# First-layer norms on ScalarE as scale and shift, and the additive part's first weights prepared beside the first chosen heads

## The chip, the cores and the metric

The kernel runs on one core of one Trainium2 chip. The metric is device time of the whole kernel in microseconds (us), the median of several runs. A core has five engines that each work through their own queue in order: TensorE (PE in the profile, with PEld for its weight loads), VectorE (DVE), ScalarE (ACT), GpSimd (POOL) and SyncE (SP, which issues DMAs here).

## The reference, cut to what matters

Input `x` is 4 x 512 x 128 in float32 (B = 4 batches, 512 tokens, width 128). Six residual blocks follow each other:

```python
x = x + 0.5 * _L0_ffn_ref(_layernorm(x), ...)   # "latent": RMS norm, 16-head causal attention, then 8 experts, top 2
x = x + _L0_attn_ref(_layernorm(x), ...)        # "full": 16-head attention without a mask
x = x + 0.5 * _L0_ffn_ref(_layernorm(x), ...)   # "latent" again
x = x + 0.5 * _L1_ffn_ref(_layernorm(x), ...)   # "chosen": per head the 64 tokens it picks
x = x + _L1_attn_ref(_layernorm(x), ...)        # "additive": 4 layers of additive attention with an MLP
x = x + 0.5 * _L1_ffn_ref(_layernorm(x), ...)   # "chosen" again
```

What the change touches are norms. A latent block takes `y = layernorm(x)` and then `h = y * rsqrt(mean(y*y) + 1e-6) * g1`; a full block takes `layernorm(x)` alone; and within a latent block, before its experts, there is a second RMS norm `y * rsqrt(mean(y*y) + 1e-6) * g2`. The additive block's weights are folded before use: products such as `Wp @ Wf`, `Wq @ Wq.T` with the norm's gain and bias worked in.

## The kernel before, in words

All of `X` (and a second copy `Y`) stays in SBUF, as 128 partitions x 4 batches x 4 chunks x 128. The function `tile_macaron` calls three parts in turn: `first_layer` (the first three blocks, interleaved), `chosen_attention`, `additive_attention`, and `chosen_attention` once more.

**First layer.** There are 12 tasks: latent, full, latent, each for four batches. `attention()` walks over all their units; a unit is four groups of heads for one chunk of queries. Each unit has two halves. In a half it issues two score matmuls for the row maxima (`maxima`, L527), two in transposed form with the maximum already subtracted (`shifted`, L562), the maxima's reduction on VectorE (`reduce_max`, L543 with a mask or L547), two exponentials on ScalarE (`exponent`, L574), the causal mask on GpSimd (`mask`, L580), the products with the values two units later (`products`, L605), and one step each of an expert's first and second product (`one_hidden`, `one_combined`, L267 with ScalarE L467, VectorE L472 and GpSimd L473). Then `step_background` runs one step of whatever generator waits: the `yield`s in the code are the ends of such steps.

Two of these generators are what the change touches. `Task.prepare` (L301 to L352) makes a task's normed input: moments on VectorE (L167, L171), variance plus epsilon (L312, L316) and the power -0.5 on GpSimd (`rsqrt`, L154), a step later the norm itself, `h`, four instructions of 128 x 128, one for each chunk (L323; on VectorE for the first task, on GpSimd for all others), a step later the transposes (L193) and their copy `hT` on ScalarE (L339 or L331). A latent task also writes the plain layernorm to `Y` in four more GpSimd instructions (L336). `gates` (L673 on) is the second RMS norm of a latent task, which GpSimd applies in four instructions (L686), followed by the top-2 choice among the experts (L703 to L737, with two GpSimd steps, L712 and L718).

PSUM has eight banks of 128 x 512; `bank()` deals them out by a written-down estimate of when each will be free. The build then orders each engine's instructions itself: an instruction written later can be put ahead of an earlier one where the build's own estimate sees that engine idle and the inputs there. On the chip each queue then runs strictly in that order.

**Chosen attention** (L858 on) picks tokens with an 8-at-a-time maximum on VectorE (L836, L838), gathers them by matmuls (L880), projects (L903), attends and adds back (L983, L992). `in_turn` runs its generators round robin: the four batches' streams, and the choice for batches 2 and 3.

**Additive attention** (L1009 on) first prepares the folded weights of layer 0 to the end (`weights(0)`: six DMAs L1035 to L1045, VectorE L1049 to L1106, TensorE L1058, L1074, L1080, L1095, L1097, L1104, ScalarE L1065 and L1084), then starts four streams five turns apart; the weights of layers 1 to 3 are prepared beside the streams. Its tiles lie in pools that open after those of the chosen attention have closed.

Of the kernel before, what the change touches and what calls it, by code (L numbers as in the profile page):

```python
# [15 lines left out]
B = 4  # L16
# [24 lines left out]
def tile_macaron(ctx: ExitStack, tc: tile.TileContext, a: dict, out: bass.AP):  # L41
# [97 lines left out]
    def in_turn(runs):  # L139

        t = 0
        while runs:
            for start, run in list(runs):
                if start <= t and next(run, 0) == 0:
                    runs.remove((start, run))
            t += 1
# [85 lines left out]
    def first_layer(opened, picked):  # L232
        with (
# [42 lines left out]
            class Task:  # L276
# [24 lines left out]
                def prepare(self):  # L301
# [15 lines left out]
                    n = 2 * NC if self.causal else NC  # L317
                    r = rsqrt(v[:, 0:n], n)
                    yield
                    eng = nc.gpsimd if self.k else nc.vector  # L320
                    for c in range(NC):
                        at = n - NC + c
                        eng.tensor_scalar(  # L323
                            h[:, c, :], X[:, b, c, :], mv[:, c, 0:1], r[:, at : at + 1], ALU.subtract, ALU.mult
                        )
                    yield
                    if self.part == "full":
                        nc.gpsimd.tensor_tensor(
                            X[:, b], X[:, b], late["a_bo"].unsqueeze(1).to_broadcast([P, NC, P]), op=ALU.add
                        )  # L330
                        nc.scalar.copy(hT, transposed(h))  # L331
                        yield
                        wq, wk, self.wv, src = late["a_wq"], late["a_wk"], late["a_wv"], hT
                    else:
                        for c in range(NC):
                            nc.gpsimd.tensor_scalar(  # L336
                                Y[:, b, c, :], X[:, b, c, :], mv[:, c, 0:1], r[:, c : c + 1], ALU.subtract, ALU.mult
                            )
                        nc.scalar.activation(hT, transposed(h), AF.Copy, scale=f_cols[:, 0:1])  # L339
                        yield  # L340
                        wq, wk, self.wv, src = f_wq, f_wkv[:, 0:P], f_wkv[:, P : 2 * P], hT
                    self.src = src
                    ps = bank()
# [329 lines left out]
            def gates(task):  # L673
# [9 lines left out]
                yield  # L683
                h = wp.tile([P, NC, P], F32, name="h")
                for c in range(NC):
                    nc.gpsimd.tensor_scalar(h[:, c, :], Y[:, b, c, :], r[:, c : c + 1], None, ALU.mult)  # L686
                yield
                nc.vector.scalar_tensor_tensor(X[:, b], Y[:, b], 0.5, X[:, b], ALU.mult, ALU.add)
                yield
# [165 lines left out]
        for i, b in enumerate(batches):  # L855
            picked[b] = ygs[i], byt[:, :, i * NE : (i + 1) * NE]

    def chosen_attention(top, picked, choosing):  # L858

        with tc.tile_pool(name="moa", bufs=2) as wp:  # L860

# [135 lines left out]
            def behind(b):  # L997

                while b not in picked or (b > 0 and steps[b - 1] < 5):
                    yield  # L1000
                for _ in stream(b):
                    steps[b] += 1
                    yield
                steps[b] += 5

            in_turn([(0, choosing)] + [(0, behind(b)) for b in range(B)] + [(0, others)])


    def additive_attention(opened, picked):  # L1009

        A = 2 * P
        with tc.tile_pool(name="add", bufs=2) as wp, tc.tile_pool(name="one", bufs=1) as hp:

            fold = hp.tile([P, P], F32, name="fold")
            nc.gpsimd.affine_select(
                out=fold,
                in_=ident,
                pattern=[[0, P]],  # L1020
                compare_op=ALU.is_ge,
                fill=-1.0,
                base=P - 2,
                channel_multiplier=-1,
            )
            hs = [hp.tile([P, NC, P], F32, name=f"hs{b}") for b in range(B)]
            for b in range(B):
                nc.gpsimd.memset(hs[b][:, :, P - 1 : P], 1.0)
            ready, finished = {}, set()

            def weights(i):

                cols = late["l_cols"][:, i, :]
                wqk = wp.tile([P, 2 * A], F32, name="wqk")
                nc.sync.dma_start(wqk, a["l_wqk"][i])  # L1035
                bqk = wp.tile([P, A], F32, name="bqk")
                nc.sync.dma_start(bqk, a["l_bqk"][i, :, 0:A])
                wpT = wp.tile([P, 2, A], F32, name="wpT")
                nc.sync.dma_start(wpT, a["l_wpT"][i].rearrange("(h p) n -> p h n", p=P))
                wfg = wp.tile([P, 2, P + 1], F32, name="wfg")  # L1040
                nc.sync.dma_start(wfg, a["l_wfg"][i].rearrange("(h p) n -> p h n", p=P))
                w1 = wp.tile([P, 4 * P], F32, name="w1")
                nc.sync.dma_start(w1, a["l_w1"][i])
                w2 = wp.tile([P, 4, P], F32, name="w2")
                nc.sync.dma_start(w2, a["l_w2"][i].rearrange("(h p) n -> p h n", p=P))  # L1045
                for _ in range(3):
                    yield
                L = wp.tile([P, P], F32, name="L")
                nc.vector.tensor_scalar(  # L1049
                    L[:, 0 : P - 1], fold[:, 0 : P - 1], cols[:, COL_G1 : COL_G1 + 1], None, ALU.mult  # L1050
                )
                nc.vector.tensor_copy(L[:, P - 1 : P], cols[:, COL_B1 : COL_B1 + 1])

                wpf = wp.tile([P, 2, P], F32, name="wpf")
                ps = bank()
                for f in range(2):
                    for k in range(2):
                        nc.tensor.matmul(  # L1058
                            ps[:, f * P : (f + 1) * P],
                            lhsT=wpT[:, k, f * P : (f + 1) * P],  # L1060
                            rhs=wfg[:, k, 0:P],
                            start=(k == 0),
                            stop=(k == 1),
                        )
                nc.scalar.copy(wpf, ps[:, 0:A].rearrange("p (f n) -> p f n", f=2))  # L1065
                yield
                bpw = wp.tile([P, 2, P], F32, name="bpw")
                for f in range(2):
                    nc.vector.tensor_scalar(
                        bpw[:, f, :], wfg[:, f, 0:P], cols[:, COL_BP + f : COL_BP + f + 1], None, ALU.mult  # L1070
                    )

                ps = bank()
                nc.tensor.matmul(ps[:, 0:A], lhsT=L, rhs=wqk[:, 0:A], start=True, stop=True)  # L1074
                wq = wp.tile([P, A], F32, name="wq")
                nc.vector.tensor_tensor(wq, ps[:, 0:A], bqk, ALU.add)
                yield
                ps = bank()
                for f in range(4):
                    nc.tensor.matmul(  # L1080
                        ps[:, f * P : (f + 1) * P], lhsT=wqk[:, f * P : (f + 1) * P], rhs=L, start=True, stop=True
                    )
                wT = wp.tile([P, 4, P], F32, name="wT")
                nc.scalar.copy(wT, by_chunk(ps))  # L1084
                nc.vector.tensor_tensor(
                    wT[:, :, P - 1], wT[:, :, P - 1], cols[:, COL_BQK : COL_BQK + 4], ALU.add
                )
                yield

                wa = wp.tile([P, A + P + 1], F32, name="wa")  # L1090
                ps = bank()
                for k in range(2):
                    for f in range(2):
                        of = wT[:, 2 * k + f, :]
                        nc.tensor.matmul(ps[:, k * P : (k + 1) * P], lhsT=of, rhs=of, start=(f == 0), stop=(f == 1))  # L1095
                for f in range(2):
                    nc.tensor.matmul(  # L1097
                        ps[:, A : A + P + 1], lhsT=wT[:, f, :], rhs=wfg[:, f, :], start=(f == 0), stop=(f == 1)
                    )
                nc.vector.tensor_copy(wa, ps[:, 0 : A + P + 1])  # L1100
                yield
                ps = bank()
                for f in range(2):
                    nc.tensor.matmul(ps[:, 0:P], lhsT=ones[:, 0:P], rhs=bpw[:, f, :], start=(f == 0), stop=(f == 1))  # L1104
                crow = wp.tile([P, P], F32, name="crow")
                nc.vector.tensor_tensor(crow, ps[:, 0:P], late["l_rows"][:, i, ROW_BF : ROW_BF + P], ALU.add)  # L1106
                ready[i] = wa, wq, wT, wpf, crow, w1, w2

            def stream(b):

# [150 lines left out]
                finished.add(b)  # L1261


            for _ in weights(0):
                pass
            STEPS = 23
            runs = [(STEPS // B * b, stream(b)) for b in range(B)]
            runs += [(STEPS * (i - 1) + 15, weights(i)) for i in range(1, DEPTH)]
# [16 lines left out]
            in_turn(runs + [(STEPS * DEPTH, chosen_beside())])  # L1285
        return top, picked, choosing

    for half in (first_layer, additive_attention):
        with ExitStack() as until_chosen:

            def opened():
                return until_chosen.enter_context(tc.tile_pool(name="top", bufs=1, side="right"))

            chosen_attention(*half(opened, {}))
    for b in range(B):
        nc.sync.dma_start(out[b].rearrange("(c p) d -> p c d", p=P), X[:, b])

# [66 lines left out]
```

## Time and profile before

| | |
|---|---|
| Median of 3 runs | 1376.09 us (1375.94 to 1377.14) |
| The profiled execution's own time | 1375.36 us |
| Span of that execution, first to last instruction | 1373.6 us |
| PE busy | 1288.2 us (94%) |
| DVE busy | 953.5 us (69%) |
| ACT busy | 587.1 us (43%) |
| POOL busy | 563.3 us (41%) |
| First layer, its units | about 17 to 815 us, the last experts until about 885 us |
| First chosen attention | about 885 to 978 us |
| Additive attention | about 978 to 1250 us |
| Second chosen attention | about 1250 to 1374 us |

Times in a trace are counted from the first instruction. A row of the timeline reads: start, length, engine, line, operation, what it writes and what it reads, shapes, how many in a row, and in brackets how long the engine had been idle before and what ended that. A row of the waits reads: who waited for whom, us in total, how often, the longest. In the table of stages, PEclk is the share of its full clock that TensorE was granted.

### The profile page before, as it was taken

The page shows a single profiled execution, that of the slowest core. Times are in us where ns is not written, and L with a number is a line of the kernel's source. Part 1 is how long each engine was busy: PE and PEld are TensorE (multiplying, and loading weights), DVE is VectorE, ACT ScalarE, POOL GpSimd, SP SyncE. Part 2 cuts the span into 40 slices and gives each one's busy share as a digit, 9 for nine tenths or more (in the row PEclk, how much of TensorE's full clock was granted, in tenths as well). Part 3 has the DMA queues.
Part 4 walks back from the last instruction along what each step waited for, and adds up shares of the span by engine and source line. Part 5 has one row for each costly group of instructions (what it writes and reads, how often), then busy time and mean ns, then how long its engine had stood idle before and what let it go on. Part 6 is the DMA issues. An engine that isn't in the chain of part 4 may idle for free.

```text
span 1373.6 us, 29346 instructions
## 1 busy us (share of the span) xinstructions
PE 1288.2 (94%) x11050; PEld 699.2 (51%) x11050; DVE 953.5 (69%) x3293; ACT 587.1 (43%) x1180; POOL 563.3 (41%) x823
## 2 busy tenths in 40 slices
PE   5998999999999999999999999989799999997897
PEld 2554444333333333465444443466667767665675
DVE  6886676666657777878767548687466776667773
ACT  1555454454546666655545443222123332323122
POOL 8345655544424202025564655622144443543100
PEclk8999999999999999999999999999969999999799
DMA  3001111020111100000101021000300000000000
GB/s 115 21 24 43 40 33 49 2 80 1 64 44 32 38 2 18 18 3 19 60 22 46 20 71 40 32 0 17 100 20 5 16 1 16 1 1 1 1 9 23
DMA packets 37172, 39.52 MB, mean 29 GB/s; under 512 B 11080, under 2 KB 23880, under 8 KB 37032
## 3 DMA queue, kind: packets, MB, share of 16 engines
q1 hardware_dynamic: 34536, 35.06, 8.1%
q10 hardware_dynamic: 2496, 2.59, 0.6%
q8 instruction: 87, 1.43, 0.4%
q14 instruction: 53, 0.43, 0.1%
HBM read 29.45 MB, written 1.18 MB: 22 GB/s over the span
## 4 chain that ended last, share of the span: by engine, by line
PE 71%; DVE 17%; POOL 9%; issue 2%; ACT 1%; DMA 0%; SPq 0%; DVEq 0%; POOLq 0%; ACTq 0%
PE bank L562 17%; PE sum L605 10%; PE bank L267 10%; PE sum L267 7%; PE bank L527 6%; POOL r L154 4%; PE bank L193 4%; PE bank L880 2%; PE bank L983 2%; DVE st L167 2%; PE bank L1250 2%; PE bank L903 1%; PE bank L1142 1%; PE bank L1244 1%; DVE junk L543 1%
## 5 line engine op out<-in xcount | busy, mean ns | idle before, releaser
L574 ACT ACTIVATE e<-bank 128x512 f32<-128x512 f32 x576 | 313.9, 595 | 276.5 <-PE bank L527 238.0
L527 PE MATMUL bank<-kA,qA 32*128 32x512 f32 (+3 forms) x1536 | 345.6, 524 | 3.8 <-DVE nm L543 1.8
L562 PE MATMUL bank<-qA,kA 32*128 32x512 f32 (+3 forms) x1536 | 331.9, 521 | 0.3 <-DVE nm L543 0.3
L543 DVE CUSTOM_DVE_ANT_0 junk<-bank,causal 128x384 f32<-128x384 f32 (+3 forms) x512 | 251.0, 490 | 88.4 <-PE bank L527 50.2
L547 DVE TENSOR_REDUCE nm<-bank 128x1 f32<-128x512 f32 x256 | 164.9, 686 | 77.4 <-PE bank L527 77.0
L473 POOL TENSOR_TENSOR hid<-v,spread 128x512 f32<-128x512 f32 x128 | 164.1, 1288 | 126.0 <-DVE v L472 101.5
L562 PEld LDWEIGHTS bank<-qA,kA 32*128 32x128 f32 x1536 | 128.5, 184 | 136.6 <-issue 54.8
L605 PE MATMUL sum<-e,vA 128*32 128x256 f32 (+1 forms) x2560 | 183.1, 367 | 7.5 <-POOL e L580 7.5
L580 POOL TENSOR_SCALAR_AFFINE_SELECT e<-e 128x256 f32<-128x256 f32 x256 | 99.7, 409 | 191.3 <-ACT e L574 190.3
L527 PEld LDWEIGHTS bank<-kA,qA 32*128 32x128 f32 x1536 | 146.0, 185 | 23.8 <-DVE nm L543 5.8
L605 PEld LDWEIGHTS sum<-e,vA 128*32 128x32 f32 x2560 | 62.7, 109 | 166.5 <-issue 133.6
L267 PE MATMUL sum<-hid,sb_f_w 128*32 128x512 f32 x1024 | 135.6, 597 | 2.8 <-POOL hid L473 2.7
L267 PE MATMUL bank<-tT,sb_f_w 128*32 128x512 f32 x1024 | 137.1, 602 | 0.0
L472 DVE SCALAR_TENSOR_TENSOR v<-th,bank 128x512 f32<-128x512 f32 x128 | 87.1, 681 | 43.3 <-ACT th L467 28.4
L467 ACT ACTIVATE th<-bank 128x512 f32<-128x512 f32 x128 | 76.4, 598 | 48.5 <-PE bank L267 39.0
L154 POOL TENSOR_TENSOR r<-v,mhalf 128x4 f32<-128x4 f32 (+1 forms) x64 | 71.9, 1125 | 5.1
L1244 PE MATMUL bank<-h2T,w 128*128 128x512 f32 x128 | 69.0, 632 | 0.2 <-ACT h2T L1233 0.2
L1250 PE MATMUL bank<-w,hid 128*128 128x128 f32 x512 | 65.6, 277 | 0.1
L1250 PEld LDWEIGHTS bank<-w,hid 128*128 128x128 f32 x512 | 62.9, 194 | 4.8 <-issue 1.5
L1245 ACT ACTIVATE hid<-bank,sb_l_cols 128x512 f32<-128x512 f32 x64 | 44.0, 689 | 40.1 <-PE bank L1244 39.8
L1142 PE MATMUL bank<-wa,hT 128*128 128x385 f32 x128 | 57.6, 547 | 2.5 <-ACT hT L1135 2.5
L312 POOL TENSOR_SCALAR v<-mv 128x4 f32<-128x4 f32 x12 | 2.8, 231 | 130.8 <-DVE mv L171 130.5
(279 smaller groups left out, 1807.9 us busy)
## 6 DMA issues: line engine op xcount, KB each, us to landing
spread<-away SPq DMA_DIRECT2D x64, 256.0 KB
qA<-mT SPq DMA_DIRECT2D x192, 2.0 KB
qA<-qC SPq DMA_DIRECT2D x11, 256.0 KB
kA<-kC SPq DMA_DIRECT2D x11, 256.0 KB
w<-in_l_w_dram SPq DMA_DIRECT2D x8, 256.0 KB
sb_m_wqkv<-in_m_wqkv_dram SPq DMA_DIRECT2D x4, 384.0 KB
m_yg<-in_m_trig_dram SPq DMA_DIRECT2D x8, 130.0 KB
X<-in_x_dram SPq DMA_DIRECT2D x4, 256.0 KB
```

The source lines that it names most:

```text
L154: last_root[0] = nc.gpsimd.tensor_tensor(r[:, 0:n], src, mhalf[:, 0:n], op=ALU.pow).ins
L267: nc.tensor.matmul(ps[32 * j : 32 * j + 32, :], lhsT=w[:, 32 * j : 32 * j + 32], rhs=rhs, start=start, stop=stop, skip_group_check=True,)
L472: nc.vector.scalar_tensor_tensor(v, th, 1.0, ph, ALU.add, ALU.mult)
L473: nc.gpsimd.tensor_tensor(hid, v, self.spread[e], op=ALU.mult)
L527: nc.tensor.matmul(ps[:, at : at + w], lhsT=t.qA[r0 : r0 + 32, g, c * P : (c + 1) * P], rhs=t.kA[r0 : r0 + 32, g, 0:w], start=True, stop=True,
L543: nc.vector.tensor_tensor_reduce(junk[:, 0:w], src, causal[:, T - w : T], 1.0, NEG, ALU.add, ALU.max, dst)
L547: nc.vector.tensor_reduce(dst, src, axis=AX.X, op=ALU.max)
L562: nc.tensor.matmul(ps[:, at : at + w], lhsT=t.kA[r0 : r0 + 32, g, kc * P : (kc + 1) * P], rhs=t.qA[r0 : r0 + 32, g, q0:T], start=True, sto ...
L574: nc.scalar.activation(es[n][:, j, :], ps, AF.Exp)
L580: nc.gpsimd.affine_select(out=e, in_=e, pattern=[[0, 2], [1, P]], compare_op=ALU.is_ge, fill=0.0, base=0, channel_multiplier=-1,)
L605: nc.tensor.matmul(to[32 * j : 32 * j + 32, q0 + lo - at : q0 + hi - at], lhsT=t.vA[:, kc, 4 * j + g, :], rhs=es[n][:, j, lo:hi], start=fresh,
L1250: nc.tensor.matmul(pm[:, c * P : (c + 1) * P], lhsT=hid[:, f, c * P : (c + 1) * P], rhs=w2[:, f, :], start=(f == 0), stop=(f == 3),)
```

## The change

It does four things.

1. In `Task.prepare`, VectorE computes `nb = -mean * r` (one instruction for a full task, two for a latent one, each 128 x 4). For every task but the first, `h` is written one step later, and by ScalarE: an activation Identity with `r` as scale and `nb` as bias.
2. For latent tasks but the first, `Y` is written by ScalarE in the same way, after the step that issues `hT`.
3. In `gates`, `h = Y * r` is written by ScalarE instead of GpSimd.
4. `weights` moves out of `additive_attention` into a function of its own, `additive_weights`, with its own pool (`made`) that opens ahead of the first chosen attention; `weights(0)` runs there from turn 8, six turns between its DMAs and its first use. The tiles `wqk`, `bqk`, `wpT`, `wfg`, `L` and `bpw` have one buffer instead of two.

```diff
-                    eng = nc.gpsimd if self.k else nc.vector
+                    nb = small.tile([P, 2, NC], F32, name="nb")
+                    for i in range(n // NC):
+                        nc.vector.scalar_tensor_tensor(
+                            nb[:, i, :], mv[:, :, 0], -1.0, r[:, i * NC : (i + 1) * NC], ALU.mult, ALU.mult
+                        )
+                    def applied(dst, i, c):
+                        at = i * NC + c
+                        nc.scalar.activation(
+                            dst, X[:, b, c, :], AF.Identity, scale=r[:, at : at + 1], bias=nb[:, i, c : c + 1]
+                        )
+                    if self.k:
+                        yield
                     for c in range(NC):
                         at = n - NC + c
-                        eng.tensor_scalar(
-                            h[:, c, :], X[:, b, c, :], mv[:, c, 0:1], r[:, at : at + 1], ALU.subtract, ALU.mult
-                        )
+                        if self.k:
+                            applied(h[:, c, :], n // NC - 1, c)
+                        else:
+                            nc.vector.tensor_scalar(
+                                h[:, c, :], X[:, b, c, :], mv[:, c, 0:1], r[:, at : at + 1], ALU.subtract, ALU.mult
+                            )
                     yield
...
-                        for c in range(NC):
-                            nc.gpsimd.tensor_scalar(
-                                Y[:, b, c, :], X[:, b, c, :], mv[:, c, 0:1], r[:, c : c + 1], ALU.subtract, ALU.mult
-                            )
+                        if not self.k:
+                            for c in range(NC):
+                                nc.gpsimd.tensor_scalar(
+                                    Y[:, b, c, :], X[:, b, c, :], mv[:, c, 0:1], r[:, c : c + 1], ALU.subtract, ALU.mult
+                                )
                         nc.scalar.activation(hT, transposed(h), AF.Copy, scale=f_cols[:, 0:1])
                         yield
+                        if self.k:
+                            for c in range(NC):
+                                applied(Y[:, b, c, :], 0, c)
...
-                    nc.gpsimd.tensor_scalar(h[:, c, :], Y[:, b, c, :], r[:, c : c + 1], None, ALU.mult)
+                    nc.scalar.mul(h[:, c, :], Y[:, b, c, :], r[:, c : c + 1])
...
-            in_turn([(0, choosing)] + [(0, behind(b)) for b in range(B)] + [(0, others)])
+            in_turn([(0, choosing)] + [(0, behind(b)) for b in range(B)] + [(0, others)] + list(beside))
...
+    def additive_weights(wp, ready):
...
-                for _ in range(3):
+            for _ in range(3 if i else 6):
                     yield
...
-            for _ in weights(0):
-                pass
...
+        chosen_first = first_layer(opened, {})
+        made = tc.tile_pool(name="made", bufs=2)
+        wp, ready = until_done.enter_context(made), {}
+        weights = additive_weights(wp, ready)
+        chosen_attention(*chosen_first, beside=[(8, weights(0))])
+    with ExitStack() as until_chosen:
+        chosen_again = additive_attention(opened, {}, weights, ready)
+        until_done.close()
+        chosen_attention(*chosen_again)
```

## The prediction

> **What bounds the kernel now.** I read the page first, then the table of stages, then TensorE's waits, and only then the timeline at the places that these named. The page's totals and its chain:
>
> ```profile
> PE 1288.2 (94%) x11050; PEld 699.2 (51%) x11050; DVE 953.5 (69%) x3293; ACT 587.1 (43%) x1180; POOL 563.3 (41%) x823
> PE 71%; DVE 17%; POOL 9%; issue 2%; ACT 1%; DMA 0%; SPq 0%; DVEq 0%; POOLq 0%; ACTq 0%
> ```
>
> TensorE is the bound; GpSimd is 41% busy and holds 9% of the chain. So work taken off GpSimd is worth only what TensorE waits for it. Stage by stage (length, then busy us of PE, PEld, DVE, ACT, POOL, then TensorE's clock):
>
> ```profile
> 108.00:116.00 8.00, 5.22 (x39) 2.61 (x40) 2.82 (x14) 1.82 (x5) 6.08 (x13) 0.57 0.00 0
> 116.00:262.00 146.00, 144.43 (x1539) 66.52 (x1539) 103.12 (x351) 73.44 (x137) 82.64 (x125) 1.00 0.12 39
> 262.00:266.00 4.00, 4.00 (x24) 0.99 (x26) 1.48 (x3) 0.26 (x1) 0.34 (x1) 0.57 0.00 0
> 640.00:665.00 25.00, 19.86 (x222) 11.11 (x218) 16.99 (x77) 11.99 (x23) 18.93 (x33) 1.00 0.01 2
> 885.00:978.00 93.00, 83.49 (x558) 64.92 (x556) 65.59 (x210) 22.65 (x83) 18.41 (x33) 0.96 0.03 7
> ```
>
> In the first layer TensorE is 99% busy (144.43 of 146) except around 108 and 640, where POOL is at 76%. Its waits over the whole span say the same:
>
> ```profile
> PE sum L605 <- POOL e L580: 7.5, 3, 3.8
> PE bank L193 <- POOL h L323: 4.4, 4, 3.5
> PE bank L1058 <- DMA wfg<-in_l_wfg_dram: 1.3, 1, 1.3
> ```
>
> The three waits on the mask `e` are one place of 3.78 us (timeline at 106.72) and two of 2.34 and 1.37 (646.84, 654.5). The first on GpSimd's timeline:
>
> ```profile
> 101.51 1.67 POOL L154 TENSOR_TENSOR r<-v,mhalf 128x8 f32<-128x8 f32 x1
> 103.30 3.15 POOL L323 TENSOR_SCALAR h<-X,mv,r 128x128 f32<-128x128 f32 x4
> 106.43 3.28 POOL L336 TENSOR_SCALAR Y<-X,mv,r 128x128 f32<-128x128 f32 x4
> 109.67 1.50 POOL L580 TENSOR_SCALAR_AFFINE_SELECT e<-e 128x256 f32<-128x256 f32 x4
> ```
>
> The masks are queued behind 6.4 us of norms, and TensorE stands still for them. The other bursts of norms, but for the start, cost no visible PE time.
>
> **The change, part by part.** *Removed from POOL:* 44 instructions L323 at 797 ns, 28 of the 32 of L336 at 797 ns and 32 of L686 at 606 ns (mean of its group, 18.9 us over 32 with overlap): 34.6 + 22.3 + 18.9 = 75.8 us. Worth of it on the path:
> - Place one: the gap of 3.78 us, and after it half the clock (0.57 over the 8 us from 108 on, so half for 6.9 us): about 1.9 us of that lie in the gap, the other 5 us run at half speed and cost about 2.5. In all 6.3 us. ScalarE's own bursts will leave about 1: 5.3 gained.
> - Place two: 2.34 + 1.37, and 1.43 at 659 behind VectorE's `rank`, which waited 3.29 us for GpSimd's queue: 5.1; 4.2 gained.
> - Start: TensorE waits 3.52 + 0.9 us at 23 to 29 for the second task's `h`. GpSimd's four take 3.15 us, ScalarE's four about 1.6, and ScalarE is idle there; but VectorE's `nb` now waits for a root that came only at 24.04, with that stage's maxima behind it. Between -3 and +4; I take -0.5.
> - The last experts (815 to 885), where L473 on POOL holds TensorE for some tenths at a time: -0.5.
>
> For the clock at place one the Trainium skill (TensorE: Matmul & The Clock Gate, "Part 1: The HAM clock gate") says that an idle window of about 3.4 us halves TensorE's clock. By that rule the gap of 3.78 costs its half clock and any remainder under 3.4 us costs none, so I would book the full 2.5 us. The rows say less: after one gap of only 1.21 us (at 260.33) the stage 262 to 266 ran at 0.57 (half for 3.4 us, worth 1.7), and after 2.34 + 1.37 + 1.43 none of 640 to 665 did. The measurement decides: a short stall may still lose as much, and I keep 1 us as left over at place one.
>
> *Added on ACT:* 72 Identity activations of 128x128 with two operands per partition and 32 with one. No such row exists, so from three that do:
>
> ```profile
> L1233 ACT ACTIVATE h2T<-bank,sb_l_cols 128x512 f32<-128x512 f32 x16 | 12.4, 778 | 34.2 <-PE bank L193 34.1
> L339 ACT ACTIVATE hT<-bank,sb_f_cols 128x512 f32<-128x512 f32 x8 | 5.5, 691 | 14.3 <-PE bank L193 14.2
> L1155 ACT COPY pq<-bank 128x129 f32<-128x129 f32 x64 | 17.1, 267 | 90.0 <-DVE ss L1145 62.4 <-PE bank L1176 13.0 <-DVE mv L171 6.8
> ```
>
> A plain copy of 512 takes 588 (L1135), so one such operand adds 103 ns and two add 190; on a 128-wide copy (270) that gives 373 and 460 ns, in a row about 90 less each, as the exponentials overlap (two of 595 in 1.09 us). A burst of four: 3 x 0.37 + 0.46 = 1.57 us for Identity (18 bursts), 3 x 0.28 + 0.37 = 1.21 for `gates` (8 bursts): 38 us in all, against 51% load of ACT in the first layer. Bounds: 0.27 each (28 us) if the operands were free, 0.60 (62 us) if nothing overlapped. Identity needs no table switch: L1233 runs between the Gelu of L1245 with only two table loads there.
>
> Here a rule speaks against the change: the Trainium skill (ScalarE: Activation LUTs, "Rules for kernel authors") sends multiply and add to VectorE. The trace has that alternative: the first task's L323 on VectorE, 340 ns, four in 1.12 us. By the rule the 26 bursts would cost 29 us of VectorE, by this change 38 us of ScalarE. But VectorE is 71% busy in 116 to 262 and ScalarE 50%, so I do not count the rule as a loss: 0.45 us per burst, in an engine with room.
>
> *Added on DVE:* 20 `nb` of 128x4, nearest row L1162 at 160 ns: 3.2 us, and 0.2 us at the very start on the path.
>
> *Added waits.* This is what decides. `nb` waits on VectorE for GpSimd's root, and in its queue stand the maxima (L543, L547) and L472; `h` waits on ScalarE for `nb` or for the root, and behind it stand the exponentials. TensorE waits for the banks that both empty. GpSimd needs 0.23 + 0.20 + 1.67 = 2.1 us for a task's root and about 1.7 for that of `gates`. Eleven prepares and eight gates make 19 such waits. From below: VectorE waited 2.17 (at 204.5) and 3.32 us (780.2) for GpSimd's `hid` with no gap in TensorE at all. From above: four waits of 0.8 us of `rank` were followed by TensorE gaps of 0.37, 1.21, 0.16 and 0.86. So 0 to 1.2 us each. I take 0.25 for each, nearer to the waits of L472, which are as long as the new ones: +5 us. The 7 bursts for `Y` find their inputs ready and are counted in this.
>
> *Weights moved.* At the start of the additive part (TensorE's timeline):
>
> ```profile
> 979.53 1.00 PE L193 MATMUL bank<-ident,hs 128*128 128x128 f32 x4 [1.38 <-DVE hs L1124]
> ...
> 983.97 1.13 PE L1058 MATMUL bank<-wfg,wpT 128*128 128x128 f32 x8 [1.34 <-DMA wfg<-in_l_wfg_dram]
> ...
> 987.09 2.85 PE L1142 MATMUL bank<-wa,hT 128*128 128x385 f32 x8
> ```
>
> The first stream's transposes end at 980.5 and its `hT` at 981.2, but its next matmul (L1142) waits until 987.09 for `wa`, behind a DMA of 4.2 us. With `wa` ready it starts at about 981.3: 5.8 us gained; the later stall of 1.24 us in `bpw` L1069 (on the chain, for layer 1's load) may go too: -6.3 in all. What it costs in the chosen part: TensorE 4.5 us (L1074 0.55, L1080 1.05, L1058 1.1, L1095 0.9, L1097 and L1104 0.9), VectorE about 2.2. Turns 14 to 18 fall after the choice's last transpose (927.67), at 930 to 947, where TensorE shows gaps of only 0.47 and 0.73. So between +1 (the gaps at 911 to 929 take it) and +4.5; I take +3.8. SP: six issues of 0.43 us, behind which only L785 stands, needed much later: 0. POOL: `fold`, 0.3 us in a stage at 20%: 0. One buffer: the loads for layer 2 wait for layer 1's last reader instead of going out at 981 to 987; a layer takes some 62 us, so 0; without that cover 4 to 6 us each. Sum: -2.5.
>
> **The sum.** -5.3 - 4.2 - 0.5 - 0.5 + 0.2 + 5 - 2.5 = -7.8 us. The profiled execution took 1375.36 us (span 1373.6 and 1.76 around it), which gives 1367.6; the median stands 0.7 higher: 1368.
>
> **The rivals.**
> - *The new in-order waits decide (slower).* Gains without them are 12.8 us; over 19 waits the change is slower from 0.67 us of TensorE per wait on. At 1.2 us: +22.8 - 12.8 = +10: 1386; near 0.85: 1379. For it: the gaps after `rank`. Against it: L472's longer waits without a gap. 0.23.
> - *Stalls change their engine (no change).* At places one and two `gates`, `h` and `Y` meet on ScalarE: 1.2 + 1.6 + 1.6 us beside its exponentials, and TensorE waits for those instead; or the weights' 4.5 us and the waits eat the rest. About 0.55 us per wait: 1374 to 1378. Against it: ScalarE is about half idle there. 0.14.
> - *Everything goes well.* No new stalls (-5), the start gains 3, the weights' full 6.3: 1376 - 22 = 1354. 0.1, as the far end of the forecast's side.
> - *It does not relieve GpSimd:* excluded, the instructions go.
>
> **How the numbers follow.** Forecast side, faster, 1354 to 1373: 0.63, of which 0.53 around 1368 (1360 to 1373). No change within 0.2% (2.75 us, about what a measurement of this kernel can tell): 0.14. Slower: 0.23, half of it over 1383. The range runs from 1354, the sum without stalls, to 1383, 0.98 us per wait; about 0.16 is left out.
>
> **What would show it.** Right: the wait of L605 on POOL at 106 and 646 gone or under 1 us, PEclk 1.00 in the fourth slice, L1142 of the first stream 2 us after its transposes, the chosen part 3 to 4 us longer, POOL near 488 us, ACT near 625. Wrong: many waits of `nb` or L574 on `r` above 1 us with TensorE gaps after them (rival one); ACT activations over 0.6 us; a first chosen part longer by 6 us or more. Since the build orders every queue anew, a place without a stall now can gain one; that would be the likeliest way to be wrong.

## The result, and the profile after

The changed kernel took 1424.42 us (median of 4 runs, 1424.23 to 1424.69); the kernel before took 1376.61 us beside it. The ratio is 1.0348, 95% interval 1.033 to 1.0366: slower by 48 us. The prediction said 1368 and a range up to 1383.

The page's first part, after; the columns are those shown of before:

```profile
PE 1325.4 (93%) x11050; PEld 712.6 (50%) x11050; DVE 956.9 (67%) x3313; ACT 622.2 (44%) x1284; POOL 487.2 (34%) x719
```

GpSimd lost its 76 us and ScalarE gained 35, as worked out (487.2 and 622.2, against 488 and 625). But TensorE, with the same 11050 matmuls, is busy 37 us longer. The table of stages says why (length, busy us of PE, PEld, DVE, ACT, POOL, then TensorE's clock); the last row is of before:

```profile
21.00:46.00 25.00, 18.39 (x68) 8.73 (x68) 16.67 (x70) 8.14 (x19) 4.20 (x11) 0.52 0.04 12
440.00:461.00 21.00, 16.27 (x88) 4.51 (x80) 9.36 (x23) 10.56 (x24) 3.58 (x5) 0.67 0.09 27
113.00:138.00 25.00, 23.51 (x168) 11.99 (x168) 13.53 (x54) 12.19 (x27) 5.09 (x12) 0.66 0.01 1
0.00:865.00 865.00, 821.83 (x7854) 359.00 (x7858) 576.96 (x1770) 463.87 (x899) 287.01 (x476) 0.95 0.11 33
...
0.00:812.00 812.00, 784.40 (x7862) 346.97 (x7866) 572.96 (x1750) 429.73 (x800) 359.94 (x576) 0.99 0.11 35
```

The last exponential of the first layer ends at about 864 instead of 810 us, and the granted clock up to there is 0.95 where it was 0.99. Three stretches of some 20 us ran at 0.52 to 0.67. TensorE's waits over the whole span:

```profile
PE bank L548 <- DVE nm L564: 12.6, 7, 6.4
...
PE bank L548 <- ACT e L595: 7.3, 4, 3.5
...
PE bank L583 <- DVE nm L564: 5.9, 3, 3.6
PE bank L583 <- DVE nm L568: 3.8, 4, 1.2
```

(L548 is L527 of before, L583 is L562, L564 and L568 are the maxima, L595 the exponential.) The waits on the masks and on GpSimd's `h` are gone. In their place TensorE waits for banks that VectorE's maxima and ScalarE's exponentials have not emptied. What these two stood for, in the stretch up to 865 us:

```profile
DVE nb L323 <- POOL r L154: 30.8, 12, 9.9
...
ACT h L707 <- POOL r L154: 14.5, 7, 2.3
...
ACT h L329 <- DVE nb L323: 12.8, 6, 5.4
...
ACT Y L329 <- DVE nb L323: 9.1, 4, 3.8
```

These are 67 us of standing in two queues, for the root; the waits of the two queues overlap in time in part. The largest is at the start. VectorE's timeline:

```profile
13.73 0.35 DVE L171 BATCH_NORM_AGGREGATE mv<-st 128x2 f32<-128x6 f32 x4
24.03 0.24 DVE L323 SCALAR_TENSOR_TENSOR nb<-mv,r 128x4 f32<-128x4 f32 x2 [9.94 <-POOL r L154]
25.64 0.23 DVE L323 SCALAR_TENSOR_TENSOR nb<-mv,r 128x4 f32<-128x4 f32 x2 [1.37 <-POOL r L154]
25.79 0.69 DVE L564 CUSTOM_DVE_ANT_0 junk<-bank,causal 128x512 f32<-128x512 f32 x1
```

`nb` of the second and of the third task stands right behind their moments, ahead of the very first maximum. GpSimd writes constants until 22, so VectorE stands until 24.03, and the maximum that began at 18.60 before begins at 25.79. TensorE has a gap of 6.44 us at 20.09. The largest later loss is a ring through four engines, at 440; three timelines, PE, ACT and POOL:

```profile
442.30 1.12 PE L548 MATMUL bank<-kA,qA 32*128 32x512 f32 x2
446.94 2.07 PE L548 MATMUL bank<-kA,qA 32*128 32x512 f32 x2 [3.52 <-ACT e L595]
```

```profile
440.50 1.65 ACT L329 ACTIVATE h<-X,nb,r 128x128 f32<-128x128 f32 x4 [1.45 <-DVE nb L323]
445.92 0.49 ACT L329 ACTIVATE Y<-X,nb,r 128x128 f32<-128x128 f32 x1 [3.77 <-DVE nb L323]
446.31 0.57 ACT L595 ACTIVATE e<-bank 128x512 f32<-128x512 f32 x1
```

```profile
442.22 1.26 POOL L345 TENSOR_TENSOR X<-X,sb_a_bo 128x512 f32<-128x512 f32 x1 [1.96 <-ACT h L329]
443.45 0.23 POOL L312 TENSOR_SCALAR v<-mv 128x4 f32<-128x4 f32 x1
443.74 0.19 POOL L316 TENSOR_SCALAR v<-mv 128x4 f32<-128x4 f32 x1
444.02 1.67 POOL L154 TENSOR_TENSOR r<-v,mhalf 128x8 f32<-128x8 f32 x1
```

GpSimd adds the bias to `X` (L345) only once ScalarE has read `X` for `h`; behind that stands the next task's root (445.69), behind that VectorE's `nb` (445.71), behind that ScalarE's `Y`, and behind `Y` the exponentials that hold TensorE's banks. After the gap two such matmuls take 2.07 us where two took 1.12, and the clock granted over this stage is 0.67.

The weights did better than forecast. From the first stream's `hs` to the second chosen attention before took 301.3 us (979.0 to 1280.4) and now 292.6 (1037.6 to 1330.2); the first chosen attention grew from 93.3 to 95.7 us. TensorE's first matmul of the first stream stands right behind the transposes:

```profile
1040.19 0.58 PE L193 MATMUL bank<-ident,hs 128*128 128x128 f32 x2 [0.81 <-DVE hs L1151]
1040.61 2.75 PE L1169 MATMUL bank<-wa,hT 128*128 128x385 f32 x8
```

### The profile page after: what moved, and what is told of

Read it like the earlier page. It is cut to its first block, busy times and chain, and to the rows that moved or that the text cites. A ratio compares the mean times of both kernels' runs of the same rounds, so it can differ in the third digit from the quotient of the medians.

```text
span 1422.9 us, 29361 instructions
## 1 busy us (share of the span) xinstructions
PE 1325.4 (93%) x11050; PEld 712.6 (50%) x11050; DVE 956.9 (67%) x3313; ACT 622.2 (44%) x1284; POOL 487.2 (34%) x719
## 5 line engine op out<-in xcount | busy, mean ns | idle before, releaser
L595 ACT ACTIVATE e<-bank 128x512 f32<-128x512 f32 x576 | 313.2, 594 | 260.1 <-PE bank L548 225.5
L548 PE MATMUL bank<-kA,qA 32*128 32x512 f32 (+3 forms) x1536 | 371.2, 547 | 22.9 <-DVE nm L564 12.6
L583 PE MATMUL bank<-qA,kA 32*128 32x512 f32 (+3 forms) x1536 | 342.6, 536 | 10.2 <-DVE nm L564 5.9
L564 DVE CUSTOM_DVE_ANT_0 junk<-bank,causal 128x384 f32<-128x384 f32 (+3 forms) x512 | 251.1, 490 | 95.4 <-PE bank L548 55.8
L568 DVE TENSOR_REDUCE nm<-bank 128x1 f32<-128x512 f32 x256 | 165.0, 686 | 88.5 <-PE bank L548 88.3
L583 PEld LDWEIGHTS bank<-qA,kA 32*128 32x128 f32 x1536 | 131.4, 189 | 146.9 <-issue 50.6
L626 PE MATMUL sum<-e,vA 128*32 128x256 f32 (+1 forms) x2560 | 187.7, 375 | 0.0
L548 PEld LDWEIGHTS bank<-kA,qA 32*128 32x128 f32 x1536 | 154.2, 193 | 56.8 <-DVE nm L564 17.5
L267 PE MATMUL bank<-tT,sb_f_w 128*32 128x512 f32 x1024 | 138.3, 606 | 0.0
L267 PE MATMUL sum<-hid,sb_f_w 128*32 128x512 f32 x1024 | 135.1, 596 | 3.3 <-POOL hid L494 3.3
```

What stands on the lines that cost most here:

```text
L267: nc.tensor.matmul(ps[32 * j : 32 * j + 32, :], lhsT=w[:, 32 * j : 32 * j + 32], rhs=rhs, start=start, stop=stop, skip_group_check=True,)
L548: nc.tensor.matmul(ps[:, at : at + w], lhsT=t.qA[r0 : r0 + 32, g, c * P : (c + 1) * P], rhs=t.kA[r0 : r0 + 32, g, 0:w], start=True, stop=True,
L564: nc.vector.tensor_tensor_reduce(junk[:, 0:w], src, causal[:, T - w : T], 1.0, NEG, ALU.add, ALU.max, dst)
L568: nc.vector.tensor_reduce(dst, src, axis=AX.X, op=ALU.max)
L583: nc.tensor.matmul(ps[:, at : at + w], lhsT=t.kA[r0 : r0 + 32, g, kc * P : (kc + 1) * P], rhs=t.qA[r0 : r0 + 32, g, q0:T], start=True, sto ...
L595: nc.scalar.activation(es[n][:, j, :], ps, AF.Exp)
```

## The experiments

**Theory 1:** the loss is in the waits themselves. The build puts the new instructions ahead of maxima and exponentials, where their input is not there yet, and the strictly ordered queues stand. **Theory 2:** the 35 us of added ScalarE work delay the exponentials by themselves. A ratio is to the kernel before in the same session, with its 95% interval; it is not the ratio of the two medians, from which it differs by up to 0.15%. Before's own median was 1373.7 to 1376.9 us in these. In the first two kernels the norms are on GpSimd as before; all others keep the changed kernel's norms but for what is said. A second measure is how late an exponential starts against the kernel before, in the profiled executions (us; the 576 exponentials have the same order in all):

| Exponential no. | 0 | 48 | 72 | 240 | 252 | 312 | 372 | 480 | 575 |
|---|---|---|---|---|---|---|---|---|---|
| changed kernel | 8.8 | 10.4 | 16.8 | 24.6 | 35.8 | 41.9 | 48.7 | 53.5 | 53.5 |
| weights_only | 0.0 | 0.0 | 0.0 | 0.0 | 0.0 | 0.0 | 0.0 | 2.7 | 0.6 |
| busy_only | 0.1 | 1.0 | 0.9 | 2.9 | 2.9 | 3.6 | 4.3 | 6.4 | 5.5 |
| nb_gpsimd | 2.2 | 2.4 | 8.7 | 18.7 | 26.4 | 33.6 | 40.8 | 45.7 | 45.9 |
| pin_act_only | 7.4 | 7.9 | 10.1 | 13.5 | 18.4 | 20.2 | 22.0 | 24.6 | 24.9 |
| pinned | 4.8 | 6.4 | 3.2 | 1.7 | 1.6 | 2.0 | 2.4 | -0.5 | -0.3 |
| pin_start | -0.1 | 0.0 | -2.4 | -3.9 | -3.9 | -3.3 | -2.9 | -5.7 | -5.2 |
| pin_rank | 0.4 | 0.5 | -6.5 | -10.4 | -10.5 | -9.8 | -9.4 | -12.2 | -16.2 |
| norms_vector | 10.4 | 12.0 | 18.1 | 37.6 | 46.1 | 52.4 | 56.9 | 64.7 | 66.2 |
| vector_pinned | -0.1 | 0.8 | -1.9 | -3.0 | -3.0 | -2.8 | -2.6 | 1.3 | 1.9 |

The changed kernel loses in steps: at the start (8.8 us), at the first change of tasks, at 440 (11.2 us, between no. 240 and 252), at two more changes of tasks in the full block, and near 692 us.

**weights_only.** All norms as before; only part 4 of the change stays.

```diff
-                        nc.scalar.activation(dst, X[:, b, c, :], AF.Identity, scale=..., bias=...)
+                        nc.gpsimd.tensor_scalar(dst, X[:, b, c, :], mv[:, c, 0:1], r[:, at : at + 1], ALU.subtract, ALU.mult)
```

> The changed kernel with all norms of the first layer back on GpSimd as before; only the additive weights stay moved. Theory 1 (in-order waits: VectorE and ScalarE stand in their queues at nb and h until GpSimd's root is there) and theory 2 (the 38 us of added ScalarE work by itself holds up the exponentials) both put the whole loss in the first layer: by the stages of the two traces the rest became 6.8 us shorter, so 1376.6 - 6.8 = about 1370, first layer ending at 885 to 887 as before. If the moved weights share in the loss: over 1380.

1370.48 us, ratio 0.9974 (0.9955 to 0.9994). The exponentials are as before to 2.7 us, the last one to 0.6 us: the whole loss belongs to the norms.

**busy_only.** Norms on GpSimd; ScalarE also does 104 activations on constants at the places of the change, into a tile that nobody reads.

```diff
+                i = nc.scalar.activation(spare, ident, AF.Identity, scale=mhalf[:, 0:1], bias=mhalf[:, 1:2])
+            tc.keep_in_program_order(i)
```

> As weights_only, and ScalarE does the 104 extra 128x128 activations at the places of the change, but on constants into a spare tile that nobody reads: the same busy time, no wait for a root. Norms stay on GpSimd. Theory 1: within 6 us of weights_only, 1370 to 1376, the start unchanged. Theory 2: most of the loss is there, 1405 to 1424.

1372.58 us, ratio 0.9969 (0.995 to 0.9989); 5.5 us late at the last exponential. Theory 2 falls: the work costs about 5 us in the first layer of this execution, not 53, and in the time of the kernel it can't be told from weights_only.

**nb_gpsimd.** `nb` on GpSimd, behind the root, from a negated mean made ahead of it.

```diff
-                        nc.vector.scalar_tensor_tensor(nb[:, i, :], mv[:, :, 0], -1.0, r[...], ALU.mult, ALU.mult)
+                        nc.gpsimd.tensor_tensor(nb[:, i, :], minus, r[...], op=ALU.mult)
```

> The changed kernel, but nb is made by GpSimd right behind the root, so VectorE waits for nothing new; ScalarE still waits for root and nb. Theory 1 in the form that VectorE's waits carry most of it: the 6.4 us gap at the start and the waits of maxima behind nb go, 1380 to 1395. In the form that ScalarE's waits carry most: 1410 to 1420. Theory 2: 1424, since ScalarE's work is the same.

1415.35 us, ratio 1.0295 (1.0257 to 1.0333): the second form. VectorE no longer stands for `nb`, which saves 6.6 us at the start and little after. ScalarE's waits without VectorE's carry 45.9 us of lateness (GpSimd's chain ahead of `h` is a little longer here, so this is rather too much); most of TensorE's waits are now for ScalarE (up to 830 us):

```profile
PE bank L548 <- ACT e L595: 11.3, 6, 3.1
```

**pin_act_only.** The reverse: ScalarE's instructions are held behind everything written before them on ScalarE (an order of issue, no wait); `nb` stays free.

```diff
-                        nc.scalar.activation(
+                        tc.keep_in_program_order(nc.scalar.activation(
```

> The changed kernel with only the ScalarE instructions (h, Y) held in their written place; nb on VectorE may still be put ahead of the maxima. Theory 1, ScalarE's waits carrying most (nb on GpSimd saved only 8 us): the places at 443, 514 and 581 go, the start stays (+9 us), 1376 to 1390. If VectorE's waits do as much once ScalarE's are gone: 1395 to 1415.

1395.0 us, ratio 1.0133 (1.0109 to 1.0158), at the edge of the second form. With VectorE's waits left, the exponentials are still 24.9 us late, 7.4 of it at the start (once GpSimd's bias add stands 29.9 us for the held `h`, so that not all of it need be VectorE's). With one queue freed at a time, VectorE's costs 25 us and ScalarE's 46, both together 53: the waits overlap.

**pinned.** `nb`, `h` and `Y` all held in their written places; the same instructions on the same engines as in the changed kernel.

> The changed kernel with the same instructions on the same engines, but each nb, h and Y of the change is held behind everything written before it on its engine, so it can't be put ahead of maxima or exponentials. Theory 1: waits for the root of over 1 us gone from VectorE and ScalarE, 1362 to 1375, the start at most 1 us longer than before. Theory 2: no change, 1415 to 1424.

1369.0 us, ratio 0.995 (0.9933 to 0.9967). This settles it: the work unchanged, only its place in the queues, and 53.8 us of lateness are gone. At the start of the changed kernel VectorE's `nb` stood ahead of the first maximum (24.03 and 25.79 above); in pinned the first maximum follows the moments directly, and `nb` stands behind the twentieth:

```profile
19.62 0.69 DVE L568 CUSTOM_DVE_ANT_0 junk<-bank,causal 128x512 f32<-128x512 f32 x1 [5.53 <-PE bank L552]
...
31.12 0.23 DVE L324 SCALAR_TENSOR_TENSOR nb<-mv,r 128x4 f32<-128x4 f32 x2
```

TensorE's waits for maxima from 40 to 812 us are down to

```profile
PE bank L552 <- DVE nm L568: 2.8, 3, 1.5
PE bank L587 <- DVE nm L568: 2.3, 2, 1.5
PE bank L552 <- DVE nm L572: 1.4, 2, 1.2
```

and there is none left for an exponential. At the start pinned still lost 4.8 to 6.4 us, where at most 1 was expected, since `h` now waited for an `nb` behind all the maxima.

**later_steps.** The changed kernel with three more steps written between the root and `nb`, and between the root and `h` of `gates`.

```diff
+                    for _ in range(3 if self.k else 0):
+                        yield
```

> The changed kernel with three more steps written between the root and its users (nb, and h in gates), nothing held in place. Theory 1, with the place in the queue set by the build's own estimate of when the root is ready and not by where it is written: nearly no change, 1412 to 1426. If the written distance decides: 1365 to 1380.

1432.91 us, ratio 1.0417 (1.0382 to 1.0451), above the interval expected: the written distance does not help. At the start `nb` waits the same 9.94 us. This fits a build that takes an instruction forward as soon as it holds its input to be ready.

**norms_vector.** `h` and `Y` on VectorE, no `nb`, not held.

```diff
-                        nc.scalar.activation(dst, X[:, b, c, :], AF.Identity, scale=..., bias=...)
+                        nc.vector.tensor_scalar(dst, X[:, b, c, :], mv[:, c, 0:1], r[:, at : at + 1], ALU.subtract, ALU.mult)
```

> The changed kernel with h and Y on VectorE (subtract and multiply, no nb), free to be put ahead. Theory 1: VectorE now stands for the root with the maxima behind it, start included, so slower than weights_only by 10 us or more: 1382 to 1410. Rival (it was ScalarE's engine choice, and VectorE is the better place): 1365 to 1373.

1439.5 us, ratio 1.0455 (1.0425 to 1.0484): worse than either side expected, and worse than ScalarE. Up to 860 us VectorE stood

```profile
DVE h L323 <- POOL r L154: 27.2, 10, 10.2
```

**vector_pinned.** The same on VectorE, held in place, with the exception of the next kernel for the second task.

> pin_start with h and Y on VectorE instead of ScalarE (no nb), held in place likewise. Theory 1 (place in the queue decides, not the engine): within 5 us of pin_start, 1362 to 1372, where norms_vector, the same work not held, took 1439.5. Rival (VectorE has no room for 29 us more): 1385 or more.

1375.85 us, ratio 1.0015 (0.9996 to 1.0034). The last exponential comes 1.9 us late where norms_vector's came 66.2 late: the place in the queue is worth some 64 us here, 10.5 of them at the start, where the exception has a part. But the expectation was missed by 4 us: at 1365.5 in the same session (pin_start_again), the ScalarE form is 10 us faster. TensorE's waits for maxima up to 830 us are only about 2 us longer than in pin_start:

```profile
PE bank L549 <- DVE nm L565: 3.7, 4, 1.9
PE bank L584 <- DVE nm L565: 3.6, 3, 1.9
```

Up to the first `pick`, which comes 9.9 us later than in pin_start_again, TensorE stands 4.3 us longer and is busy at half clock for 8.6 us longer, worth another 4.3. Half of the 10 us is thus clock; that VectorE lacks room is not shown.

**pin_start** and **pin_start_again.** pinned, with the second task's `h` and `Y` on GpSimd as before and no `nb` for the first two tasks.

```diff
+                        if self.k == 1:
+                            nc.gpsimd.tensor_scalar(dst, X[:, b, c, :], mv[:, c, 0:1], r[:, at : at + 1], ALU.subtract, ALU.mult)
+                            return
...
-                    for i in range(n // NC):
+                    for i in range(n // NC if self.k > 1 else 0):
```

> pinned, with the second task's h and Y back on GpSimd and no nb for the first two tasks. pinned lost 6 us at the start, where h waited for an nb behind all the maxima of the first stage (TensorE gap 2.84 us). Theory 1: the start as before, 1369 - 5 = 1362 to 1366. If pinned's start cost was covered later anyway: 1368 to 1370.

> The kernel of pin_start once more, beside the other two on one chip: 1364 to 1368, ratio to the kernel before 0.990 to 0.995.

1366.99 us, ratio 0.9925 (0.9899 to 0.9951), and again 1365.47, ratio 0.9926 (0.9899 to 0.9952). The first was expected at 1362 to 1366 and missed it by 1 us. The start is as before (-0.1 us), and the last exponential is 5.2 us early.

**pin_rank.** pin_start, and VectorE's `rank` in `gates`, an instruction of the kernel before, held in place too.

```diff
-                nc.vector.tensor_reduce(rank, more, axis=AX.X, op=ALU.add)
+                tc.keep_in_program_order(nc.vector.tensor_reduce(rank, more, axis=AX.X, op=ALU.add))
```

> pin_start, and the reduction rank in gates (there in the kernel before as well, L725) also held in its written place. It waits 0.8 us for GpSimd's more in most tasks and TensorE gaps of 0.36 to 1.56 follow: at 109, 178, 260, 328, 651 and 720 they sum to 5.6 us, with half clock after three. Theory 1 (any instruction put ahead of its input costs so): 3 to 8 us under pin_start, about 1361. If those gaps have another cause: within 2 us of pin_start.

1361.49 us, ratio 0.9896 (0.9871 to 0.9921): the best version, 4 us under pin_start_again by the medians (the intervals of the two ratios overlap slightly). TensorE's longest waits from 40 to 812 us, in pin_start and then in pin_rank:

```profile
PE bank L557 <- DVE nm L573: 2.8, 3, 1.6
PE bank L592 <- DVE nm L573: 1.5, 1, 1.5
PE bank L557 <- DVE nm L577: 1.4, 2, 1.2
```

```profile
PE bank L193 <- DVE o L435: 1.0, 4, 0.5
PE bank L401 <- DVE nm L573: 0.5, 1, 0.5
PE bank L592 <- DVE nm L577: 0.3, 1, 0.3
```

The three waits for maxima were `rank`'s doing, and the last exponential comes 16.2 us earlier than before. But the first `pick` comes only 5.0 us earlier: the experts at the end of the first layer give 11 us back. There the held `rank` has a price of its own: the last one starts 13.5 us after GpSimd's `more` has ended (0.6 us in pin_start_again), behind the choice of tokens on VectorE, and TensorE stands 5.03 us for the choice's `slot`, 1.41 for `comb` and 2.40 for `hid`, where pin_start_again has no such gap above 0.80; 17 us between 820 and 861 run at half clock. Of the 4 us to pin_start_again, the profiled executions show 1.1 at the first `pick`; the rest lies behind the first layer, where the kernels are alike, so that the hit within 3 to 8 us was partly luck.

## Why the prediction was wrong, by its own steps

The row that the failed term rests on, with what stood behind it, in VectorE's timeline of before:

```profile
204.51 0.69 DVE L472 SCALAR_TENSOR_TENSOR v<-th,bank 128x512 f32<-128x512 f32 x1 [2.17 <-POOL hid L473]
205.11 0.68 DVE L543 CUSTOM_DVE_ANT_0 junk<-bank,causal 128x512 f32<-128x512 f32 x1
```

- **"So 0 to 1.2 us each. I take 0.25 for each."** This term failed, and with it the sign. It was booked at +5 us; pinned against the changed kernel gives 53.8 us of lateness in the first layer for those 19 waits, 2.8 us each on average, over twice the upper bound. The rival named the right mechanism, new in-order waits, with too small a price. Three things were wrong in the working.
  - *The nearest row.* I took the waits of L472 for `hid` (2.17 and 3.32 us, no gap), because they were as long. Behind the first two maxima stood, as behind the new waits, but TensorE had 3 us of other matmuls to do (203.1 to 206.1: L267, L605, L193); behind the second no maximum stood. So these rows showed one wait that other work covered. Some of the new ones cost next to nothing too: at 178 and 267, where ScalarE alone waited 2.1 us, TensorE had no gap over 0.3 us behind it and the exponentials came no later than by 0.4 us. `rank` was the row whose wait did cost (0.8 us, then up to 1.2), and my bound took waits of about 2 us as no dearer.
  - *Two queues at once.* I counted a wait per task; VectorE waits for the root, ScalarE for VectorE, and GpSimd (L345) for ScalarE. At 440 such waits of 1.10, 1.45, 3.38 and 3.77 us stand within 6 us, and TensorE's gaps there are 1.20 and 3.52. nb_gpsimd and pin_act_only price the two queues at 46 and 25 us alone.
  - *The clock.* By the two rows of the first layer above, TensorE's idle time rose from 27.6 to 43.2 us and its busy time by 37.4. Its time at half clock rose from 20.5 to 85.3 us; it was busy for 14.2 and 75.2 of these, and busy time at half speed costs half of itself, so the clock accounts for about 30 us: 15.6 + 30.5 = 46 of the 53. I had kept 1 us for a stall left over at place one and no clock for the 19 waits. The remaining 7 us are not attributed.
- **"Start: between -3 and +4; I take -0.5."** Measured +8.8. I had both numbers, the root at 24.04 and in the trace the maxima from 18.60 on, and did not subtract them: with `nb` ahead of the first maximum, VectorE's maxima would be 5.4 us late and all that follows them. The bound assumed that it stood between them.
- **Where the queue puts an instruction.** I read steps in the code as distance, and named the build's new order only as a risk. The trace of before had the sign: `rank` is written two steps behind `more`, and stood ahead of those steps' maxima. later_steps shows that written distance buys nothing.
- **Places one and two: right in mechanism.** TensorE's waits on the mask are gone; in pin_start the gaps of 3.78 and of 2.34 + 1.37 are replaced by 1.47 and 1.55, which are `rank`'s. Their sizes were too large: half clock still follows place one for 6.8 us (0.72 from 108 to 120 us), and pin_start gains there 2.4 us of the 5.3; only with `rank` held is the clock 1.00 and the gain 6.5 (exponential no. 72).
- **The rule on VectorE against ScalarE.** Rightly set aside: held in place, VectorE's form is 10 us slower. That room on the engine is the reason, as I argued, is not shown. Not held, both fail.
- **ScalarE's cost: right.** 481 ns for Identity and 390 for one operand, against 460 and 373:

```profile
L329 ACT ACTIVATE h<-X,nb,r 128x128 f32<-128x128 f32 x44 | 18.1, 481 | 12.8 <-DVE nb L323 12.8
L707 ACT ACTIVATE h<-Y,r 128x128 f32<-128x128 f32 x32 | 10.4, 390 | 17.3 <-POOL r L154 17.3
```

- **Weights: right in sign, too small.** Forecast -2.5 (+3.8 and -6.3); by the stages +2.4 and -8.7; weights_only as a whole is 0.26% faster.
- **"Everything goes well": 1354.** The three terms named there, on top of the sum, make 19 us and not 22, so 1357.

With the order held, the forecast's total was about right (pinned 1369.0, pin_start 1367.0 and 1365.5, forecast 1368), but in part by luck: in pinned the first `pick` comes 1.0 us later than before, where -5.3 was forecast for the first layer, and what follows is 6.9 us shorter, where -2.5 was. Nor does it save the forecast: the order is part of what was built.

## What to carry to other kernels

When work moves to an engine that serves the bottleneck, ask first what will stand behind it in that queue while its input is missing, and price the wait by that. Where a build orders the queues by its own estimate, written distance is no protection; hold the instruction in place and measure both ways, for a held instruction can stand behind other work, as `rank` did for 13 us. Short stalls of TensorE cost more than their length when the clock drops behind them (here 15.6 us of idle time and about 30 us of clock).

## What the runs showed of the hardware that was not expected

Time at half clock comes in steps of about 3.4 us (3.4, 6.8, 10.2, 13.7 in the changed kernel's first layer) and can long outlast the stall: with the 6.44 us gap at 20 it became half for 23.9 us, from 21.7 on, and TensorE was busy 18.01 of the last 19.09 us of these:

```profile
26.54:45.63 19.09, 18.01 (x64) 8.69 (x68) 15.26 (x62) 5.70 (x14) 0.00 (x0) 0.50 0.05 16
```

The Trainium skill (TensorE: Matmul & The Clock Gate, "Part 1: The HAM clock gate") gives a window of 3.4 us, which agrees with the steps; its idle window as the condition does not cover the halving after gaps of 0.84 and 1.79 us at 578 to 581 (half from 581.5 for 6.8 us).
